# One standing PSUM tile for the products of the update stage

## The chip, the cores and the metric

The kernel runs on one core of one Trainium2 chip. The metric is device time in microseconds from the start to the end of one execution. Engines are named as in the profile: PE (TensorE, with PEld for its weight loads), DVE (VectorE), ACT (ScalarE), POOL (GpSimd) and SP (SyncE, which issues most transfers).

## What is computed

Two layers of a graph network over 6250 nodes with 160 features (64 scalars and 32 vectors of three components) and 100,000 edges sorted by their target node. In each layer every edge makes a message from its source node's features, and the messages are summed per target node. The first layer ends with an update of each node by a full tensor product of its own features with the summed messages, and the change lies in that update:

```python
def _tp(x0, x1, y0, y1, w000, w011, w101, w110):
    out0 = (jnp.einsum('eu,ev,uvw->ew', x0, y0, w000)
            + INV_SQRT3 * jnp.einsum('euk,evk,uvw->ew', x1, y1, w110)) / np.sqrt(fan0)
    out1 = (jnp.einsum('eu,evk,uvw->ewk', x0, y1, w011)
            + jnp.einsum('euk,ev,uvw->ewk', x1, y0, w101)) / np.sqrt(fan1)
...
agg = jax.ops.segment_sum(msgs, row, num_segments=N)
a0, a1 = _split(agg)
x0, x1 = _split(node_features)
u0, u1 = _tp(x0, x1, a0, a1, wu000, wu011, wu101, wu110)
ud0, ud1 = _lin(x0, x1, lu0, lu1)
return node_features + _merge(u0 + ud0, u1 + ud1)
```

## The kernel before

The program has three stages, one after the other. scatter() makes the first layer's messages and writes them to DRAM in the order of their source bins. update() sums them per node, computes the tensor product above and prepares the tables of the second layer. windows() does the second layer. A fourth part, general(), is for inputs that don't fit the layout; it isn't executed here.

update() takes the nodes in 13 groups, twelve of 500 and one of 250, with the nodes of a group along the free axis. Its order on PE, DVE, ACT and POOL is the order in which the code issues the instructions (manual_schedule, line 952); each engine works its own list in order, and engines wait for each other through semaphores only. The framework derives those waits itself: from a tile pool, whose slot is given to a new tile when all users of the old one are done, and from the overlap of what instructions read and write in one tile.

For each group there are 32 **rounds**, listed in plan (lines 784 to 787): 8 of kind y, 16 of kind x and 8 of kind v. Sorted by their times they come as y, x, v, x, and so on. A round is Group.first (lines 828 to 863):

- It takes a PSUM tile y of 128 partitions and two banks (line 832), from the pool py, which has two such slots (line 636). So rounds alternate between two slots, four banks in all.
- PE makes two products, one into each bank. In a y round they are two fp32 matmuls on half the rows each (line 835), in an x or v round two bf16 matmuls with a one-hot matrix that repeats rows of x (line 854).
- DVE multiplies them by the summed messages a. In a y round there are two instructions (line 839): the first reads bank 0 three times over, the second bank 1. In an x or v round one instruction reads both banks (line 857). The results go to SBUF (pr, pr2).
- POOL adds what belongs together (lines 842 and 862); line 824 makes a part of the v rounds' sums ahead of time.

The result of a round is multiplied by the weights and summed on PE in out0 and out1 some rounds later (Group.second, line 870; an x round's 2 rounds later, a y round's 4, a v round's 8). Between the rounds, the loop at lines 972 to 1000 puts in pieces of two other jobs: the segment sums of the next group (sums, lines 696 to 759, with PE at lines 735 and 751) and the end of the group before (back, lines 877 to 949, with PE at lines 896, 897, 932, 942 and 943, and DVE at lines 900 to 914). A group's first two sums are opened by begin (lines 806 and 807).

PSUM has eight banks, and update() uses all: four for y, two for out0 and out1 (pool pu), two for the other jobs (pool pt).

Of the kernel before, what the change touches and what calls it, by code (L numbers as in the profile page):

```python
# [13 lines left out]
F32 = mybir.dt.float32  # L14
# [6 lines left out]
PSUM = bass.MemoryType.PSUM  # L21
DRAM = bass.MemoryType.DRAM

P = 128
# [32 lines left out]
def gnn_kernel(ctx: ExitStack, tc: tile.TileContext, a: dict, out: bass.AP):  # L57
# [565 lines left out]
    def update():  # L623
# [3 lines left out]
        with ExitStack() as s:  # L627
# [5 lines left out]
            prod = s.enter_context(tc.tile_pool(name="prod", bufs=4))  # L633
            pair = s.enter_context(tc.tile_pool(name="pair", bufs=5))
            pprod = s.enter_context(tc.tile_pool(name="pprod", bufs=2))
            py = s.enter_context(tc.tile_pool(name="py", bufs=2, space=PSUM))
            pu = s.enter_context(tc.tile_pool(name="pu", bufs=1, space=PSUM))
            pt = s.enter_context(tc.tile_pool(name="pt", bufs=2, space=PSUM))
            f0, f1 = 1.0 / math.sqrt(5120.0), 1.0 / 64.0
# [137 lines left out]
                return x0, x1, x1k, x3, v3  # L777

            halves = (slice(0, M0), slice(M0, P))

# [7 lines left out]
            class Group:  # L790
# [37 lines left out]
                def first(self, kind, c):  # L828

                    n, a = self.n, self.a  # L830
                    x0, x1, x1k, x3, v3 = self.side
                    y = py.tile([P, 2, 4 * P], F32, name="y")
                    if kind == "y":
                        for i, (half, rhs) in enumerate(zip(halves, (x0[:, :n], a[halves[1], 0, :n]))):
                            nc.tensor.matmul(y[:, i, :n], w1[half, c], rhs, start=True, stop=True)  # L835
                        prs = []
                        for i, other in enumerate((a[:, 1:, :n], x1k[:, :, :n])):
                            pr = prod.tile([P, 3, 4 * P], F32, name="pr")
                            nc.vector.tensor_tensor(pr[:, :, :n], y[:, i, None, :n].to_broadcast([P, 3, n]), other,  # L839
                                                    op=OP.mult)  # L840
                            prs.append(pr[:, :, :n])
                        nc.gpsimd.tensor_tensor(prs[0], prs[0], prs[1], op=OP.add)  # L842
                        return [(prs[0], 1, [(slice(M1 * k, M1 * k + M1), s1[:, 28 - 4 * c:][:, :M1])
                                             for k in range(3)])]
                    if kind == "v":
                        k, c = c
                    for i in range(2):
                        if kind == "x":
                            u = 2 * (c + i)
                            w, rhs = pick[:, u % M1:u % M1 + 2], x3[:, u // M1, :n]  # L850
                        else:
                            u = 4 * (c + i)
                            w, rhs = pickv[:, u:u + 4], v3[:, k, :n]
                        nc.tensor.matmul(y[:, i, :n], w.rearrange("p i v -> p (i v)"), rhs, start=True, stop=True)  # L854
                    pr = pair.tile([P, 2, 4 * P], F32, name="pr2")
                    j = 0 if kind == "x" else 1 + k
                    nc.vector.tensor_tensor(pr[:, :, :n], y[:, :, :n], a[:, j, None, :n].to_broadcast([P, 2, n]),  # L857
                                            op=OP.mult)
                    if kind == "x":
                        return [(pr, 0, list(zip(halves, (w000[:, c], w000[:, c + 1]))))]  # L860
                    pp = self.early[c]
                    nc.gpsimd.tensor_tensor(pp[:, :, :n], pp[:, :, :n], pr[:, :, :n], op=OP.add)  # L862
                    return [(self.early.pop(c), 0, list(zip(halves, (w110[:, c], w110[:, c + 1]))))] if k else []
# [819 lines left out]
    with tc.tile_pool(name="early", bufs=1) as pool:  # L1683
        e = early(pool)
        update()
        windows(e)
# [93 lines left out]
```

## Time and profile before

| | |
|---|---|
| median of 17 runs | 3767.79 us (3754.69 to 3779.67) |
| the profiled execution | 3761.49 us, span 3759.6 us |
| first and last instruction on tile y | 1406.2 and 2325.4 us |
| busy between 1405 and 2327 us | PE 829.4, DVE 704.3, POOL 680.7, ACT 371.3 us |
| granted clock of PE, in that stretch and in all | 0.97 and 0.744 |
| L854 matmuls (x and v rounds), median | 374 ns, 624 of them |
| L835 matmuls (y rounds), median | 579 ns, 416 of them |
| L839 readings (y rounds), median | 1721 and 1710 ns, 104 each |
| L857 readings (x and v rounds), median | 1192 ns, 312 |

Times are counted from the start of the span. A reading here is an instruction of DVE that reads y. An fp32 matmul appears as two entries in the trace, so the 208 matmuls of the y rounds are 416. The last group's instructions are half as wide and shorter than these medians. The clock is given as the share of full speed that PE was granted.

### The profile page before, as it was taken

What the parts mean: (1) busy time and instruction counts of PE and PEld (TensorE: products, weight loads), DVE (VectorE), ACT (ScalarE), POOL (GpSimd) and SP (SyncE); (2) the same over time, 40 slices, a digit from 0 to 9 for tenths busy, and PEclk for the clock granted to TensorE, in tenths of its full rate; (3) what the DMA queues carried; (4) which work ended last, traced back from release to release, by engine and by line L of the source; (5) the groups of instructions that cost most, each with busy time, mean ns of one, the idle gap of its engine ahead of it and who ended that gap; (6) DMA issues with size and microseconds to landing.
All of it is one profiled execution on the core that took longest, in us unless ns stands there. A gap on an engine that the chain in (4) does not pass through costs nothing.

```text
span 3759.6 us, 47528 instructions
## 1 busy us (share of the span) xinstructions
PE 2384.6 (63%) x11860; PEld 1250.4 (33%) x11860; DVE 2219.7 (59%) x4577; ACT 1525.1 (41%) x5063; POOL 2221.2 (59%) x1864
## 2 busy tenths in 40 slices
PE   5655565565544437989898998455555555655555
PEld 3433343343333322333333333132323223332323
DVE  6665555555444437867777785455555556555554
ACT  3554544454444423443443441333433333333333
POOL 3655556555666636767777776655555555555552
PEclk7777777676666658999999998566656676566656
DMA  5655555465444456666566642445444454445442
GB/s 163 180 167 163 154 161 174 148 170 152 136 131 129 136 180 179 185 191 177 172 197 192 171 136 73 131 130 147 131 136 135 131 146 134 132 134 147 133 134 74
DMA packets 352776, 563.34 MB, mean 150 GB/s; under 512 B 66034, under 2 KB 251824, under 8 KB 346603
## 3 DMA queue, kind: packets, MB, share of 16 engines
q1 hardware_dynamic: 235496, 296.85, 28.6%
q0 software_dynamic: 87584, 218.31, 19.7%
q10 hardware_dynamic: 29411, 45.06, 3.7%
q8 instruction: 96, 1.57, 0.2%
q14 instruction: 189, 1.55, 0.1%
HBM read 418.16 MB, written 133.04 MB: 147 GB/s over the span
## 4 chain that ended last, share of the span: by engine, by line
PE 23%; another core or an unknown queue 21%; ACT 15%; DVE 14%; issue 12%; DMA 7%; SPq 5%; POOL 2%; ACTq 1%; DVEq 0%; POOLq 0%
ACT wm L1093 4%; ACT junk L556 4%; PE pmsg L545 3%; PE out L870 3%; DVE pr L839 2%; PE wbank L1150 2%; PE wbank L1218 2%; PE rank L544 2%; DVE wtb L1107 2%; PE rank L543 2%; ACT uhot L719 2%; PE wgate L1081 2%; PE y L835 1%; DVE wm L1117 1%
## 5 line engine op out<-in xcount | busy, mean ns | idle before, releaser
L563 POOL DMA_INDIRECT msgs<-rec,pos_i x782 | 782.8, 1001 | 568.4 <-issue 220.3
L1062 POOL DMA_INDIRECT wgot<-T,src_i x782 | 741.5, 948 | 636.4 <-issue 425.7
L543 PE MATMUL rank<-seen,every 128*128 128x256 f16 x782 | 265.0, 339 | 459.5 <-ACT junk L556 367.6
L556 ACT ACTIVATE junk<-rank,off 128x256 bf16<-128x256 f32 x782 | 373.6, 478 | 387.7 <-remote 289.5
L545 PE MATMUL pmsg<-tw,d 120*128 120x160 f32 x1564 | 470.8, 392 | 68.7 <-issue 54.9
L1081 PE MATMUL wgate<-wrad,wblk 97*128 97x480 f32 x522 | 367.6, 836 | 173.4 <-issue 140.8
L842 POOL TENSOR_TENSOR pr<-pr 128x1500 f32<-128x1500 f32 (+1 forms) x104 | 338.0, 3250 | 155.0 <-DVE pr L839 155.0
L857 DVE TENSOR_TENSOR pr<-y,a 128x1000 f32<-128x1000 f32 (+1 forms) x312 | 352.3, 1154 | 101.4 <-PE y L854 100.9
L1099 DVE TENSOR_TENSOR whot<-lane,wbank 128x192 f32<-128x192 f32 x131 | 45.9, 350 | 619.7 <-ACT wbank L1207 552.2
L1218 PE MATMUL wbank<-wms,whot 128*32 128x160 f32 x1564 | 250.1, 404 | 208.6 <-ACT wo L1222 105.3
L545 PEld LDWEIGHTS pmsg<-tw,d 120*128 120x128 f32 x1564 | 322.6, 256 | 137.2 <-issue 79.5
L1093 ACT ACTIVATE wm<-wgot,wattr 128x160 f32<-128x160 f32 x782 | 311.6, 398 | 34.7 <-DMA wgot<-T,src_i 10.8
L560 DVE CAST pos_i<-pos 128x4 int32<-128x4 f32 x196 | 42.9, 219 | 401.9 <-ACT junk L556 376.9
L1096 ACT ACTIVATE wsg<-wgate 128x480 f32<-128x480 f32 x259 | 137.4, 567 | 350.0 <-remote 189.5
L544 PEld LDWEIGHTS <-upto 128*128 128x128 bf16 x782 | 93.0, 119 | 552.6 <-issue 508.4
L1218 PEld LDWEIGHTS wbank<-wms,whot 128*32 128x32 f32 x1564 | 144.5, 142 | 395.4 <-ACT wo L1222 136.4
L862 POOL TENSOR_TENSOR ppr<-ppr,pr 128x1000 f32<-128x1000 f32 (+1 forms) x104 | 232.3, 2234 | 70.3 <-DVE pr L857 70.2
L531 DVE TENSOR_TENSOR seen<-seen,hot 128x256 f16<-128x256 f16 x782 | 230.5, 295 | 63.2 <-DVE hot L528 18.6
L544 PE MATMUL rank<-hot,upto 128*128 128x256 bf16 x782 | 266.4, 341 | 1.1 <-DVE hot L528 1.1
L528 DVE TENSOR_SCALAR hot<-binb,qb 128x256 bf16<-128x256 bf16 x782 | 243.7, 312 | 0.0
L839 DVE TENSOR_TENSOR pr<-y,a 128x1500 f32<-128x1500 f32 (+1 forms) x104 | 172.5, 1659 | 98.4 <-PE y L835 69.6
L1081 PEld LDWEIGHTS wgate<-wrad,wblk 97*128 97x128 f32 x522 | 128.1, 278 | 307.5 <-issue 242.6
(214 smaller groups left out, 4430.4 us busy)
## 6 DMA issues: line engine op xcount, KB each, us to landing
urec<-msgs SPq DMA_DIRECT2D x250, 322.0 KB
attb<-in_attr SPq DMA_DIRECT2D x48, 960.0 KB
tw<-T0s SPq DMA_DIRECT2D x391, 75.0 KB
xb<-hT SPq DMA_DIRECT2D x192, 125.0 KB
dstb<-in_dstrow SPq DMA_DIRECT2D x48, 480.0 KB
T0s<-tt ACTq DMA_DIRECT2D x11, 1200.0 KB
msgs<-rec,pos_i POOLq DMA_INDIRECT x782
wgot<-T,src_i POOLq DMA_INDIRECT x782
```

Of the source, the lines that this page charges most:

```text
L543: nc.tensor.matmul(rank[:, j % 2], every, before, start=True, stop=False)
L544: nc.tensor.matmul(rank[:, j % 2], upto, hot, start=False, stop=True)
L545: nc.tensor.matmul(prs[-1][:, j % 2, :F], ds[j // WP][:, j % WP], tws[j // WP], start=True, stop=True)
L556: nc.scalar.activation(junk, rank, AF.Relu, bias=off, accum_out=pos[:, j:j + 1])
L563: nc.gpsimd.indirect_dma_start(out=views[(t0 + j) % NV][:, :], out_offset=bass.IndirectOffsetOnAxis(ap=pos_i[:, j:j + 1], axis=0), in_=rec ...
L839: nc.vector.tensor_tensor(pr[:, :, :n], y[:, i, None, :n].to_broadcast([P, 3, n]), other, op=OP.mult)
L842: nc.gpsimd.tensor_tensor(prs[0], prs[0], prs[1], op=OP.add)
L857: nc.vector.tensor_tensor(pr[:, :, :n], y[:, :, :n], a[:, j, None, :n].to_broadcast([P, 2, n]), op=OP.mult)
L1062: nc.gpsimd.indirect_dma_start(out=got[u][:, i], out_offset=None, in_=T1[:, :], in_offset=bass.IndirectOffsetOnAxis(ap=src_i[:, t0 + i:t0 ...
L1081: nc.tensor.matmul(p[:, :n], blocks[u // CH][:, u % CH], rad[:, lo * F:lo * F + n], start=True, stop=True)
L1093: nc.scalar.activation(m[:, b, j:j + F], g[:, i, oS1:oS1 + F], AF.Copy, scale=attr(u)[:, i, 0:1])
L1218: nc.tensor.matmul(state["acc"][j:j + WN], hot[:, i], ms[:, i], start=t0 + i == w * WT, stop=t0 + i == end, tile_position=(0, j))
```

## The change

The pool py gets one slot in place of two, and one tile of four banks is taken from it before the rounds begin. A round takes the first or the second two banks of that tile in turn, where before it took a new tile from the pool. Matmuls, readings and their order are the same, and so is the number of banks.

```diff
-            py = s.enter_context(tc.tile_pool(name="py", bufs=2, space=PSUM))
+            py = s.enter_context(tc.tile_pool(name="py", bufs=1, space=PSUM))
...
             halves = (slice(0, M0), slice(M0, P))
+            ys, turn = py.tile([P, 2, 2, 4 * P], F32, name="y"), [0]
...
                     x0, x1, x1k, x3, v3 = self.side
-                    y = py.tile([P, 2, 4 * P], F32, name="y")
+
+                    y = ys[:, turn[0] % 2]
+                    turn[0] += 1
                     if kind == "y":
```

## The prediction

> **What bounds the kernel now.** I read the page first: the engines' shares, then the slices, then the stretch in which the changed tile lives.
>
> ```profile
> PE 2384.6 (63%) x11860; PEld 1250.4 (33%) x11860; DVE 2219.7 (59%) x4577; ACT 1525.1 (41%) x5063; POOL 2221.2 (59%) x1864
> ...
> PE   5655565565544437989898998455555555655555
> ...
> DVE  6665555555444437867777785455555556555554
> ...
> PEclk7777777676666658999999998566656676566656
> ```
>
> No engine is full over the span, but slices 16 to 24 stand out: PE at nine tenths, DVE at seven to eight, the clock at 0.9. That is the update stage. The instructions on tile y run from 1406.2 us to the last reading at 2325.4 (0.65 long): 919.8 us. Nothing of the next stage's compute runs beside it, so a microsecond more in it is a microsecond more in the span.
>
> Then the waits in that stretch (engine, line, what it waited for: us, times, longest):
>
> ```profile
> DVE pr L857 <- PE y L854: 100.9, 94, 4.2
> DVE pr L839 <- PE y L835: 69.6, 71, 3.1
> ...
> PE y L854 <- DVE pr L839: 32.6, 40, 10.2
> PE y L835 <- DVE pr L857: 12.8, 21, 0.8
> ```
>
> PE and DVE hold each other up: DVE waits 170.5 us for products, PE waits for DVE to empty a buffer. The stage is a loop of the two, and what it costs depends on how far PE may run ahead. The timeline shows that (start, duration, engine, line):
>
> ```profile
> 1860.40 0.58 PE L854 MATMUL y<-x,pick 96*128 96x500 bf16 x2
> ...
> 1861.03 1.20 DVE L857 TENSOR_TENSOR pr<-y,a 128x1000 f32<-128x1000 f32 x1 [0.89 <-PE y L854]
> ...
> 1861.91 0.68 PE L835 MATMUL y<-x,w_f 64*128 64x500 f32 x1
> ...
> 1862.95 1.04 PE L870 MATMUL out<-pr,s 128*32 128x500 f32 x6
> ...
> 1863.13 1.72 DVE L839 TENSOR_TENSOR pr<-y,a 128x1500 f32<-128x1500 f32 x1 [0.91 <-PE y L835]
> ...
> 1863.92 0.59 PE L854 MATMUL y<-x,pick 96*128 96x500 bf16 x2
> 1864.44 1.06 PE L870 MATMUL out<-pr,w_f 128*64 128x500 f32 x4
> ...
> 1864.77 1.71 DVE L839 TENSOR_TENSOR pr<-y,x1k 128x1500 f32<-128x1500 f32 x1
> ...
> 1866.40 1.19 DVE L857 TENSOR_TENSOR pr<-y,a 128x1000 f32<-128x1000 f32 x1
> ...
> 1866.54 0.59 PE L854 MATMUL y<-v,pickv 96*128 96x500 bf16 x2 [0.29 <-DVE pr L839]
> ```
>
> At 1863.92 PE makes the next round's products while DVE reads the y round's (1863.13 to 1866.48); so DVE goes on at 1866.40 without a gap. Two rounds on, the v round's matmuls (1866.54) wait for both readings.
>
> **The change, step by step.** It adds no computing instruction and removes none. The same four banks are used; what changes is who waits for whom.
>
> *1. What the bookkeeping sees.* Before, each round's y is a tile of its own from a pool of two. After, all 416 rounds use one tile, and the order is kept by the overlap of accesses inside it. So the question is whether two accesses to different banks of one PSUM tile count as overlapping. Three facts of the program before say yes. In a y round the first L839 reads bank 0 alone, yet it waits for the count raised by the second matmul, which writes bank 1 (in 80 of 104 rounds the first matmul raises no count at all). The second L839, which alone needs bank 1, has no wait on PE. And in wm, the other two-bank tile, each L1093 into the second bank is ordered behind those into the first. Both are two-bank tiles; none of four exists before. I take it that a PSUM tile is ordered as a whole.
>
> *2. The wait that follows.* Then the two halves of the standing tile are no double buffer. The first matmul of a round waits for the last reading of the round just before, not of the one two rounds back. Behind it on PE's queue stand all L870 sums, the segment sums (L735, L751) and the transposes; DVE waits for the products. Products and readings strictly alternate. From the timeline: a y round is 1.22 us from first matmul to first reading (1861.91 to 1863.13), 3.35 of readings (to 1866.48), 0.06 until PE starts again: 4.63. An x or v round is 0.63 (1860.40 to 1861.03), 1.20 and 0.06: 1.89. Four rounds y, x, v, x: 4.63 + 3 x 1.89 = 10.30. There are 104 such fours; in the last group eight have 250 columns, and from their shortest rows (readings 0.94, 0.93 and 0.65) I estimate 6.0. Sum 96 x 10.30 + 8 x 6.0 = 1036.8, which is **117 us** over the 919.8.
>
> *3. Waits the alternation doesn't hold.* DVE also waited for transfers: 17.9 us for a at the start, 21.6 for uxo, 9.2 for x1k. The first stays, the others shrink as rounds get longer and the DMA does not: between 18 and 49, I take **30**.
>
> *4. PE late.* In an x round PE is done with the products 0.52 us after their start (1863.92 to 1864.44) and needs 0.99 for its L870 pair (to 1865.43); 0.38 of the 1.89 is left. Segment sums come as sets of 1.23 us, 58 of them, two fifths in the first x round: 23 x 0.85 = 20. The group's opening matmuls (L806, L807: 1.9 us) come in a v round, 13 x 1.0 = 13; a few of L942 and L943 besides. I take **40**. The ends: 0, and 120, if three fifths of those lines' 265 us came late but for the 0.38s. POOL is no limit: 3.25 + 2.23 + half of 2.24 is 6.6 per four rounds.
>
> *5. PE's clock.* While DVE reads a y round, PE has its own L870 sums (to 1863.99) and then nothing of the rounds until 1866.48: a hole of 2.49 us. What such a hole does can be read in the trace (stretch: PE busy, PEld, DVE, ACT, POOL, clock, DMA share, GB/s):
>
> ```profile
> 1616.70:1620.10 3.40, 1.24 (x10) 1.07 (x11) 2.45 (x2) 0.53 (x2) 2.29 (x2) 1.00 0.55 198
> 1620.10:1623.60 3.50, 3.50 (x14) 1.92 (x16) 0.59 (x1) 2.12 (x4) 2.47 (x1) 0.51 0.46 117
> ...
> 2087.80:2091.20 3.40, 1.25 (x7) 0.66 (x7) 2.21 (x3) 0.00 (x0) 0.63 (x1) 1.00 0.67 122
> 2091.20:2094.60 3.40, 3.40 (x30) 1.33 (x32) 3.26 (x4) 0.00 (x0) 3.40 (x2) 0.50 0.02 5
> ```
>
> The clock changes on a grid of 3.4 us; where PE was busy for 1.25 of a cell, the next ran at half. The hole behind the second was 2.50 us (L896 waiting for L900). The stage has eight such drops, after cells with 0.9 to 2.1 of 3.4 busy, while cells with 1.96 and 1.91 (from 1838.6 and 2057.0) kept the clock. So a cell with over 1.5 us of hole drops. A hole of 2.49 thrown on the grid puts that much into one cell in (0.92 + 1.98) / 3.41 = 85% of the cases. Some 60 of the 104 y rounds have no segment sums or transposes to fill the hole; with some of the filled ones I take 65 drops. In a half-speed cell an x round needs 1.04 + 2.0 = 3.0 us of PE instead of 1.89, so 3.41 us do 1.1 rounds and not 1.8: 1.3 us lost; as the clock came back only after a cell that was busy throughout, 1.7 cells each, 2.2 us. 65 x 2.2 = **143**. The ends: 0 (the eight drops of now), and 104 x 2.5 = 260.
>
> The Trainium skill (TensorE: Matmul & The Clock Gate, "Why this matters for your kernels") warns only of PE-idle gaps above about 3 us. By that rule a hole of 2.49 would cost nothing and the sum would end near 3955; the 2.50 us hole above speaks against it, and the row decides.
>
> *6. What is saved.* Even with the whole tile ordered, nothing: no wait of before becomes shorter, since the round just before always ends later than the one two back.
>
> **Sum.** 117 + 30 + 40 + 143 = 330. The profiled execution took 3761.5 us for a span of 3759.6: 3761.5 + 330 = 4091.5. The median of the runs, 3767.8, is 6 above it: **4098**, and I write 4100.
>
> **Rivals.**
>
> *A. The banks are freed one by one (faster).* The price is in the v rounds only: x and v rounds read both banks with one instruction, a y round with two. The v round's first matmul could start 1.65 us earlier (1864.77 instead of 1866.48), the second not. So PE saves at most one matmul's spacing, 0.22 to 0.30, in the rounds in which it waited: 94 by PE's and PEld's counts (40 and 54), 21 to 28 us; half of it, where the next x round waits for its own buffer anyway (0.51 at 1867.64), 12. Time 3768 - 20 = 3748. It decides as soon as accesses to different banks of a tile are kept apart. For it: at 1863.92 a matmul and a reading run side by side in different banks, so the chip allows it. Against: step 1. Chance 0.04.
>
> The Trainium skill (PSUM — Partial Sum Buffer, "Summary: rules for kernel authors") says to read PSUM beside a matmul from a different bank and to guard it by bank. By that the sum would be this rival's 3748; the waits in this program are coarser than the rule.
>
> *B. The slots stay apart, the banks in one do not.* Then every wait is as before: 3768. No tile of four banks exists before, so I can't exclude it. Chance 0.05.
>
> *C. Whole tile, but the clock holds*, because sums and transposes fill the holes or the grid treats them kindly: steps 2 to 4 alone, 117 + 30 + 40 = 187, with up to 60 of step 5: 3955 to 4015. Chance 0.28.
>
> *Forecast*, whole tile with the clock falling often: 0.63.
>
> **How the numbers follow.** Low end: steps 2 and 3 with their least, 117 + 18, and a little of step 4: 3768 + 155, 3920. High end: 117 + 49 + 80 + 225, 4240. Forecast and C lie mostly within, A and B (0.09) outside, and perhaps a tenth of the rest. A measurement of this kernel can tell about 0.2%, 7.5 us, from no change. Faster: A, 0.04. Same: B, 0.05. Slower: 0.91.
>
> **What would show it.** Right: in the stage no L854 or L835 starts before the last reading of the round before has ended; DVE's wait for y grows from 170 to 300 us or more; four rounds take 10.3 us or more where none is filled; the clock of the stage falls from 0.97 to 0.75 or 0.85; the stages before and after stay as long. Wrong: matmuls still run under L839 (A or B); a v round's first matmul starts between the two readings (A); the clock stays above 0.95 (C). If the stage grows by far more than 400 us, PE is late more often than in step 4.

## The result and the profile after

The changed kernel takes **4060.51 us** (median of 8 runs, 4041.92 to 4066.79) against 3764.52 for the kernel before on the same chips: a ratio of 1.0782, 95% interval [1.0766, 1.0798]. The prediction was 4100, range 3920 to 4240. The profiled execution has a span of 4053.4 us, 293.8 more than before. The tile y is in use from 1413.3 to 2621.6 us, 1208.3 us in place of 919.8, so 288 us of the difference lie in the update stage; the stretch ahead of it is 7.1 us longer than before and the one behind it 1.8 shorter.

The lines of its page that answer to those of before; three lines of code were added, so lines from 833 on have numbers higher by 3, those from 780 to 831 by 1:

```profile
PE 2486.1 (61%) x11860; PEld 1278.8 (32%) x11860; DVE 2237.0 (55%) x4577; ACT 1521.5 (38%) x5063; POOL 2218.4 (55%) x1864
...
PE   5555555654444367777777777735566555655556
...
DVE  6655554554444355655666656535555555555554
...
PEclk7766777666666688888889988856666666666666
```

The counts of instructions are the same. The stage now fills slices 14 to 25, and in it all three rows are lower than before: PE at seven tenths and not nine, DVE at five to six, the clock at 0.8 to 0.9. Nothing got more work; the engines wait more. (PE's total rises by 101 us with the same matmuls, since those at half clock last longer: four of L873 took 1.93 us at 1900.15, in a stretch at half clock, and 1.06 at 1906.78.)

The waits in the stage (engine, line, what it waited for: us, times, longest):

```profile
DVE pr L860 <- PE y L857: 300.5, 300, 4.2
DVE pr L842 <- PE y L838: 149.2, 94, 3.1
...
PE y L857 <- DVE pr L842: 141.4, 94, 11.9
PE y L857 <- DVE pr L860: 93.7, 130, 1.7
```

Before, the last of these was:

```profile
PE y L854 <- DVE pr L857: 8.3, 18, 0.5
```

DVE waited for x and v products 94 times before; now it does in 300 of 312 rounds, three times as long. PE's matmuls wait for the readings of an x or v round 130 times, where it was 18 times. The timeline shows the new order:

```profile
1906.27 0.58 PE L857 MATMUL y<-x,pick 96*128 96x500 bf16 x2
...
1906.96 1.20 DVE L860 TENSOR_TENSOR pr<-y,a 128x1000 f32<-128x1000 f32 x1 [1.50 <-PE y L857]
...
1908.21 0.68 PE L838 MATMUL y<-x,w_f 64*128 64x500 f32 x1 [0.37 <-DVE pr L860]
...
1909.37 1.72 DVE L842 TENSOR_TENSOR pr<-y,a 128x1500 f32<-128x1500 f32 x1 [1.21 <-PE y L838]
...
1911.01 1.71 DVE L842 TENSOR_TENSOR pr<-y,x1k 128x1500 f32<-128x1500 f32 x1
...
1912.77 0.58 PE L857 MATMUL y<-x,pick 96*128 96x500 bf16 x2 [2.48 <-DVE pr L842]
...
1913.39 1.20 DVE L860 TENSOR_TENSOR pr<-y,a 128x1000 f32<-128x1000 f32 x1 [0.67 <-PE y L857]
```

The x round's reading ends at 1908.16, the y round's matmuls start at 1908.21; the last y reading ends at 1912.72, the next x matmuls start at 1912.77. No matmul on y lies under a reading any more. The hole is there too: PE stood for 2.48 us before 1912.77 (2.49 in the prediction).

### The profile page after: what moved, and what is told of

The parts are those of the page before. It is cut to its first block, busy times and chain, and to the rows that moved or that the text cites. A ratio compares the mean times of both kernels' runs of the same rounds, so it can differ in the third digit from the quotient of the medians.

```text
span 4053.4 us, 47424 instructions
## 1 busy us (share of the span) xinstructions
PE 2486.1 (61%) x11860; PEld 1278.8 (32%) x11860; DVE 2237.0 (55%) x4577; ACT 1521.5 (38%) x5063; POOL 2218.4 (55%) x1864
## 4 chain that ended last, share of the span: by engine, by line
PE 30%; DVE 23%; another core or an unknown queue 19%; issue 11%; ACT 10%; DMA 3%; SPq 2%; POOL 1%; ACTq 1%; DVEq 0%; POOLq 0%
DVE pr L842 8%; DVE pr L860 6%; PE y L857 4%; PE out L873 4%; PE pmsg L545 4%; ACT wm L1096 3%; ACT junk L556 3%; PE y L838 3%; PE wbank L1221 2%; PE wbank L1153 2%; PE rank L544 2%; PE wgate L1084 2%; PE rank L543 2%; DVE wtb L1110 2%
## 5 line engine op out<-in xcount | busy, mean ns | idle before, releaser
L860 DVE TENSOR_TENSOR pr<-y,a 128x1000 f32<-128x1000 f32 (+1 forms) x312 | 361.7, 1159 | 300.5 <-PE y L857 300.5
L857 PE MATMUL y<-x,pick 96*128 96x500 bf16 (+1 forms) x416 | 128.4, 392 | 221.1 <-DVE pr L842 141.4
L873 PE MATMUL out<-pr,w_f 128*64 128x500 f32 (+1 forms) x832 | 243.3, 667 | 0.0
```

The costliest lines, as they stand in the source:

```text
L873: nc.tensor.matmul(out[part, :self.n], w, pr[:, i, :self.n], start=k in self.fresh, stop=self.left[k] == 0)
```

## The experiments

The theory: accesses are ordered by the whole PSUM tile, so one standing tile of four banks is a single buffer, and the loss is the alternation of products and readings, PE coming late in short rounds, and PE's clock. Rivals: that a standing tile as such costs time; that banks do overlap and something else is slow; that the clock costs nothing. A drop below is a stretch in which PE was granted half of its clock, and half-speed time is the sum of these stretches in the stage. The views have the line numbers of each run's own kernel; the text uses those of the kernel before, where it doesn't say otherwise.

### Two standing tiles

```diff
-            ys, turn = py.tile([P, 2, 2, 4 * P], F32, name="y"), [0]
+            ys, turn = [py.tile([P, 2, 4 * P], F32, name=f"y{i}") for i in range(2)], [0]
...
-                    y = ys[:, turn[0] % 2]
+                    y = ys[turn[0] % 2]
```

> The four banks stand as two tiles of two banks each, taken once and used in turn; no slot is ever given back, as in the change. Theory (accesses are ordered by the whole PSUM tile, so what hurts is that both halves are one tile): the waits are those of before, the y stage is 920 us and the time 3765 us, within 0.3%. Rival (standing tiles as such cost time, whatever their number, because no slot is released): 4060 us as with the change. Third possibility: something between, if standing tiles and the joint order both count.

Measured: 3766.27 us, ratio to before 0.9998 [0.9977, 1.0020]. The waits in its stage:

```profile
DVE pr L860 <- PE y L857: 99.7, 92, 4.3
DVE pr L842 <- PE y L838: 71.0, 71, 2.7
...
PE y L857 <- DVE pr L842: 34.6, 40, 11.9
```

They are those of before, to a microsecond or two. The banks, the order of instructions and the standing are as in the change; only the border between two tiles is new, and with it the whole loss is gone. The first rival falls.

### One slot

```diff
-            py = s.enter_context(tc.tile_pool(name="py", bufs=2, space=PSUM))
+            py = s.enter_context(tc.tile_pool(name="py", bufs=1, space=PSUM))
```

This is the kernel before with half the PSUM for y and no other edit.

> The kernel before with one slot in the pool py in place of two, so a plain single buffer of two banks. Theory (the change amounts to a single buffer): the same time as the change, 4060 us within 0.5%, stage 1208 us with about 40 clock drops. Rival (the change still overlaps some bank with some reading): the single buffer is slower than the change by 20 us or more, some 0.2 us in each of 104 y rounds.

Measured: 4049.01 us, ratio 1.0759 [1.0716, 1.0802], which holds the change's 1.0782. Its stage is 1197.5 us with 40 clock drops (the change: 1208.3 and 41).

```profile
DVE pr L857 <- PE y L854: 296.2, 300, 4.2
DVE pr L839 <- PE y L835: 138.4, 92, 3.2
```

A plain single buffer of two banks waits as the change does with four. So the other two banks buy nothing, and no bank of the standing tile is freed ahead of another to any use.

### Filling PE's hole with narrow matmuls, six and three

```diff
+                        for _ in range(6):
+                            nc.tensor.matmul(side1[0][V:, :n], pick[:, 0, :M1], x3[:, 0, :n], start=True, stop=True,
+                                             tile_position=(0, V))
                         prs = []
```

side1[0] is the group's out1, made 128 partitions high; the matmuls are added work into its unused quarter.

> The change, with six matmuls more in each y round, into a quarter of the out1 bank that nothing reads, issued just behind the y round's two products: some 1.3 us of PE work in the 2.49 us hole that PE has while DVE reads. Theory (part of the loss is PE's clock, lost in those holes): half-speed time in the stage falls from 271 us to under 80 us, and the time by 70 to 140 us, to 3920 to 3990 us, although PE does more. Rival (the clock drops fall into time in which PE waits anyway and cost nothing; all of the loss is the alternation): 4060 us or a little more.

> As with six, but three more matmuls, some 0.65 us: the hole shrinks to about 1.85 us. Theory (a 3.4 us cell of the clock's grid with over 1.5 us of hole drops): between the change and the run with six, half-speed time 130 to 230 us, time 4000 to 4050 us. Rival (only holes near 2.5 us and longer drop the clock): three do as much as six. Rival without a clock term: 4060 us.

Measured: 4044.56 us, ratio 1.0759 [1.0708, 1.0809], with six, and 4054.92, 1.0788 [1.0743, 1.0833], with three; half-speed time 259 and 317 us. Both are like the change, and neither theory is tested: the narrow matmuls ran beside the L870 sums and filled almost nothing. In the run with six, the y round of this stretch still left PE 2.04 us idle where it was 2.48.

### Filling it with full-width matmuls, six and nine

```diff
             halves = (slice(0, M0), slice(M0, P))
+            spare = pf.tile([P, 4 * P], F32, name="spare")
...
+                        for _ in range(6):
+                            nc.tensor.matmul(spare[:, :n], pick[:, 0:2].rearrange("p i v -> p (i v)"), x3[:, 0, :n],
+                                             start=True, stop=True)
                         prs = []
```

These stand on the one-slot kernel, which leaves two PSUM banks free; the tile spare is one of them and nothing reads it.

> The kernel with one slot (4049 us, half-speed time 242 us, 40 drops) plus six matmuls of full width in each y round, into one of the two PSUM banks that it leaves free and that nothing reads. The earlier fillers were a quarter wide and ran beside L870, so the hole stayed at 2.0 us; these can't, and cut it from 2.49 to some 1.1 us. Theory (lost clock is part of the loss): half-speed time under 100 us and 50 to 110 us less time, 3940 to 4000 us, with more work done. Rival (the drops cost nothing, or the added matmuls cost as much as the clock gives): 4049 us or more.

> The same with nine matmuls, 2.0 us, which fill the hole nearly whole. Theory: the clock holds (half-speed time under 60 us), but in the y rounds with segment sums or transposes PE now comes late by up to 1 us: 3950 to 4030 us, no better than with six. Rival (no clock term): slower than one slot alone by 10 to 60 us.

Measured: 4041.14 us, ratio 1.0740 [1.0722, 1.0758], with six; 4059.33, 1.0772 [1.0749, 1.0795], with nine. Half-speed time fell from 242 to 140 and 91 us, less far than expected (under 100 and under 60), and the time hardly moved. By itself that would speak for the rival. But the rounds of the trace show a second effect: in the first x rounds at full clock PE came 0.06 us after the last reading with one slot, 0.43 with six and 0.78 with nine, because in y rounds that hold segment sums there was no hole left. 90 rounds by 0.37 is 33 us. Gain and loss are mixed; the pair alone is inconclusive.

### Filling only the empty holes

The same matmuls, seven of them, at the end of a y round, and only where the loop put no segment sums or transposes in. The count at building time was 41 of 104 rounds.

```diff
+                    if kind == "y" and not busy[0]:
+                        for _ in range(7):
+                            nc.tensor.matmul(spare[:, :gs[g].n], pick[:, 0:2].rearrange("p i v -> p (i v)"),
+                                             gs[g].side[3][:, 0, :gs[g].n], start=True, stop=True)
+                    busy[0] = 0
```

> One slot, with seven matmuls of full width only at the end of those y rounds into which the loop puts no segment sums or transposes: 41 of 104. So they lie in a hole of 2.49 us and delay nothing, which those of the runs with six and nine did not (x rounds came 0.4 to 0.7 us late there). Theory (the clock costs what the half-speed rounds are longer than the others, 53 us in the profile of one slot): half-speed time from 242 us to 80 to 140, time 25 to 50 us under one slot's 4049, 4000 to 4025 us. Rival (the drops cost nothing): 4049 us. Second rival (they cost the 2.2 us each of the prediction): below 3990 us.

Measured: **3983.11 us**, ratio 1.0584 [1.0558, 1.0610], against 1.0759 for one slot: more work on PE and 66 us less time. Between the two profiled executions it is 63.2 us, of which 51.6 lie in the stage; the rest lies in the stretches around it, where the kernels don't differ. The stage by stretches (length, busy PE, PEld, DVE, ACT, POOL, clock, DMA share, GB/s), first one slot, then with the empty holes filled:

```profile
1411.00:2610.00 1199.00, 923.01 (x5258) 311.29 (x5256) 723.70 (x676) 370.45 (x1361) 682.49 (x260) 0.90 0.45 129
```

```profile
1408.00:2555.00 1147.00, 923.12 (x5550) 321.79 (x5550) 723.66 (x676) 370.95 (x1364) 682.74 (x260) 0.96 0.46 135
```

PE has some 290 matmuls more and is busy just as long, since they run at a higher clock (0.96, not 0.90). Drops fell from 40 to 17, half-speed time from 242 to 92 us, the stage from 1197.5 to 1145.9: 51.6 us for 23 drops, **2.2 us a drop**. That is more than the theory's 25 to 50 us, which came from comparing half-speed rounds with others (perhaps a slow round also delays the round behind it; this isn't shown). The second rival held: 2.2 us a drop, and a time below its 3990. The clock costs time; the first rival falls. The price comes from one pair of profiled executions, but it also fits the runs with six and nine. Six: 12 drops fewer are 27 us less, the 90 late rounds 33 more, so the stage should be 6 us longer than with one slot, and it is 4 (1201.6). Nine: 22 drops fewer are 49 less, 95 late rounds by 0.73 are 69 more, so 20 longer, and it is 19 (1216.5).

### Single banks that really come free one by one

```diff
-            py = s.enter_context(tc.tile_pool(name="py", bufs=2, space=PSUM))
+            py = s.enter_context(tc.tile_pool(name="py", bufs=4, space=PSUM))
...
-                    y = py.tile([P, 2, 4 * P], F32, name="y")
+                    y = [py.tile([P, 4 * P], F32, name="y") for _ in range(2)]
...
-                    nc.vector.tensor_tensor(pr[:, :, :n], y[:, :, :n], a[:, j, None, :n].to_broadcast([P, 2, n]),
-                                            op=OP.mult)
+                    for i in range(2):
+                        nc.vector.tensor_tensor(pr[:, i, :n], y[i][:, :n], a[:, j, :n], op=OP.mult)
```

The control has the split readings (the last lines) on the two-bank tiles of before.

> Four PSUM tiles of one bank each, two per round, and the one reading of an x or v round split into one per bank, so that the banks really come free one by one. Theory (the joint order of the tile is all that stood in the way; the first rival of the prediction named 12 to 28 us for it): faster than the kernel with two-bank tiles and split readings by 20 to 60 us, as each matmul waits for the reading of its own bank alone; against the kernel before, whose readings are not split, 3720 to 3775 us. Rival (PE and DVE are so coupled that the earlier bank gains nothing): the same as the control within 0.3%.

> The control: the kernel before with its two-bank tiles in two slots, only the one reading of each x and v round (1.19 us) split into one per bank (0.65 us each by the half-width rows, so 0.1 us more per round, 31 us in 312 rounds). Theory: DVE, which waits for PE 170 us in the stage, hides part of it: 3765 to 3800 us. Rival (the split costs in full and the second reading also delays the slot's release): 3800 us or more.

Measured: single banks 3772.92 us, ratio 1.0028 [1.0016, 1.0040]; control 3769.05, 1.0017 [1.0000, 1.0034]. The theory's 20 to 60 us are not there, and the rival holds: the earlier bank gains nothing. PE's waits, first with single banks, then in the control:

```profile
PE ptr L896 <- DVE uxo L900: 29.5, 17, 5.1
PE y L854 <- DVE pr L839: 20.1, 17, 9.9
```

```profile
PE y L854 <- DVE pr L839: 33.1, 37, 11.7
...
PE ptr L896 <- DVE uxo L900: 12.9, 10, 4.5
```

The wait for the y readings does shrink, from 37 times to 17, but behind L900, which waits for the transfer of uxo, PE now stands 16.6 us longer. That suggests the gain was given back there, which the next pair was to test.

### Loading the nodes' rows earlier

```diff
+                    if r == 24:
+                        gs[g].rows()
...
-                    xo = pool.tile([P, 4, F], F32, name="uxo")
-                    transfer(nc.sync, xs, xo, r0, n)
-                    yield
+                    xo = self.xo
+                    yield
```

rows() takes the tile uxo and loads it. The first run is the kernel before with this edit, the second has the single banks too.

> The kernel before, only the load of the nodes' rows (uxo) issued in round 24 of its own group and not when the group's end begins. Control for the next run. DVE waited 21.6 us for that transfer, PE 10.1 behind it. Theory (that wait is on the loop of PE and DVE): 3735 to 3755 us. Rival (PE or DVE waits somewhere else instead): 3765 us within 0.2%.

> Four one-bank tiles with split readings, and the early load of the rows. With four tiles alone PE's wait for the y readings fell from 33.1 to 20.1 us against the control, but the wait for uxo rose from 25.4 to 36.9 us on DVE and from 12.9 to 29.5 on PE. Theory (what the banks give is given back at that transfer): with the load early it shows, 15 to 40 us less than the early load alone, 3705 to 3735 us, faster than both kernels. Rival (the loop gains nothing from single banks, and pays for the split): the same as the early load alone, or up to 15 us more.

Measured: 3782.97 us, ratio 1.0051 [1.0034, 1.0069], with the early load alone, and 3774.24, 1.0036 [1.0019, 1.0053], with single banks too. Both expectations of a gain were wrong, and the early load alone is even slower than its rival said (within 0.2%). PE's waits with the early load alone:

```profile
PE ptr L945 <- ACT utt L950: 38.4, 10, 4.1
PE y L858 <- DVE pr L843: 32.3, 38, 10.3
```

The wait for uxo is gone from the list, but PE now waits 38.4 us for ACT's copies of utt, which take the last results of the group's end out of PSUM (6.1 before), and DVE's wait for products rises from 170 to 212 us. Whether the banks' gain went to the uxo wait therefore stays open: taking that wait away made another. Single banks were worth nothing without the early load; with it they are 9 us below, but the two intervals overlap, and the 15 to 40 us of the theory are not there.

### Moving PE's other work into the y rounds

```diff
-                    for _ in range((2, 2, 0, 1)[r % 4] if r >= 3 and g + 1 < len(groups) else 0):
+                    for _ in range((4, 0, 0, 1)[r % 4] if r >= 3 and g + 1 < len(groups) else 0):
...
-                    for _ in range((1, 2, 0, 1)[r % 4]):
+                    for _ in range((3, 0, 0, 1)[r % 4]):
```

> The change, with the two pieces of segment sums and the two of the group's end that the loop issues in each first x round moved to the y round before it; nothing else. So PE has them in the hole of 2.49 us and not in the 0.4 us that an x round leaves. Theory (PE late is a term of its own, some 44 us in the v rounds that follow those x rounds, and the clock drops come of empty y rounds): the time before the matmuls of those v rounds falls from 0.68 us to near 0.1, fewer y rounds are empty, drops fall from 41 to under 25: 40 to 90 us less than the change, 3970 to 4020 us. Rival (the moved pieces wait for each other, for ACT's copies of ptr, and PE stands in order behind them): no gain, 4050 us or more.

Measured: 4190.03 us, ratio 1.1130 [1.1108, 1.1152], so 130 us slower than the change. The moved effect is as expected where it was aimed: at full clock the v rounds' matmuls now come 0.14 us after the last reading, not 0.68. But the rival is right about the whole:

```profile
PE ptr L945 <- ACT utt L950: 90.0, 20, 9.0
```

```profile
1906.47 8.53 SPq L693 DMA_DIRECT2D urec<-msgs  x8
...
1915.11 7.40 SPq L951 DMA_DIRECT2D T<-utt  x4
1919.16 0.48 ACT L950 COPY utt<-ptr 128x384 f32<-128x384 f32 x1 [9.45 <-DMA T<-utt]
...
1919.69 0.70 PE L945 MATMUL ptr<-w_fn,uT 64*116 64x96 f32 x2 [8.79 <-ACT utt L950]
```

Issued one behind the other, the end pieces wait for ACT's copy, the copy for the transfer of an earlier piece, and all that stands behind on PE waits too. The rival didn't name one link: that transfer began to be issued only at 1915.11, since from 1906.47 to 1915.00 SyncE issued the eight loads of urec that the moved segment sums ask for. Drops rose to 63.

## Why the prediction was right

**The bookkeeping (step 1)** was right, and on it all else hung: two tiles give 0.9998, one slot gives the change's time. The chance of 0.91 for slower rested on a reading of two-bank tiles only; for four banks the same holds.

**The terms of the sum** against what the trace and the runs give:

| | predicted, us | measured, us |
|---|---|---|
| alternation (step 2) | 117 | 107 |
| waits for transfers (step 3) | 30 | 11 |
| PE late (step 4) | 40 | 65 |
| PE's clock (step 5) | 143 | 92 |
| sum | 330 | 275 |
| the stage's growth | | 288 |

- *Alternation.* At full clock a y round is 1.18 + 3.35 + 0.05 = 4.58 us and an x round 0.62 + 1.20 + 0.05 = 1.87, so a four 10.19; a half-size four is 6.03. 96 and 8 of them make 1026.5, 107 over 919.8.
- *Transfers.* DVE waits 17.8 us for a, once. The stage's first matmul starts at 1413.3 and its reading at 1425.7, 12.4 us for the usual 1.2, so 11 us of it are added to the alternation. The nine waits for x<-hX (11.6 us, 1.29 each) add next to nothing: 1.21 us is what DVE waits in a y round anyway. Those for x1k and uxo are gone.
- *PE late.* In the rounds at full clock, the time from the last reading to the first matmul is 80.6 us in sum over 315 rounds, 65 beyond the usual 0.05 each. 44 of it is in the full-size v rounds behind the first x rounds, where step 4 had put only the segment sums (20 us).
- *Clock.* **This was the mis-sized term.** The price of a drop was right (2.2 us predicted and measured). The number was not: 41 drops for the 65 predicted. Two parts of that count failed. "Some 60 of the 104 y rounds have no segment sums or transposes": it is 41. And a hole of 2.49 us was to cost a drop in 85% of the cases: filling those 41 holes took away 23 of 40 drops, 56%. As the 1026.5 us hold no drop, all 41 count, and 41 by 2.24 us are 92. The price was measured on the one-slot kernel and is carried over.

Of the 13 us that are left of the stage's growth, about 10 are in the v and second x rounds: their time from matmul to reading is 0.06 to 0.08 us longer than in the first x rounds. The 92 can be held against the change's own trace: the 101 rounds that half speed touches between the reading before and their own are 96 us longer in sum than the alternation gives (the wait for a apart), of which some is PE late.

**Too much on the clock, the transfers and the alternation and too little on PE late** cancelled in part, so the forecast lay only 40 us high; that is luck. Of the signs named, DVE's wait for y came (449.7 us in sum), and two missed by little: an unfilled four takes 10.19 us, not 10.3 or more, and the stage's clock is above the forecast's.

**Nothing saved (step 6)** fits: no term of the growth is negative. **Rival A** was wrong not only in its condition but in its price: with banks apart, 12 to 28 us were named, and none appeared. **Rival B** is ruled out by the result, since two banks apart from the other two would have left 3768. **Rival C** was nearer than its chance of 0.28 says: the stage's clock is 0.89, between its 0.95 and the forecast's 0.75 to 0.85, and 4060 lies between its 4015 and the forecast.

**The rule that step 5 names from the Trainium skill** (TensorE: Matmul & The Clock Gate, "Why this matters for your kernels": no PE-idle gap above about 3 us) would have given 3955. Holes of 2.5 us did drop the clock here, and the stage was 51.6 us shorter when the empty ones were filled, so the row of the trace was the better guide.

## What to carry to other kernels

Before merging buffers into one standing PSUM tile, look at what the program orders by: if a reader of one bank waits for the writer of another bank of its tile, the tile is the unit, and two tiles of the same banks keep the overlap that one tile loses. When two engines come to alternate, count not only the gap between them but also what the idle engine's other work does, late in short rounds and missing in long ones, and whether the holes cost it its clock. A wait that is taken away in a loop of several engines may come back somewhere else, so its length is no forecast of the gain.

## What the runs showed of the hardware

- In the prediction's rows PE's clock fell to half after a 3.4 us cell with a hole of 2.50 us, and each drop cost 2.2 us of time in the one-slot stage. Not every such hole did it: filling 41 of them took 23 drops away. And half-speed time is not all lost time: 150 us less of it (242 to 92) made the stage 51.6 us shorter.
- A matmul of 32 columns into one quarter of the partitions runs beside matmuls into the others: six of them left 2.04 us of a hole of 2.48.
- Splitting a reading of 128x1000 into two of 128x500 cost DVE little: two took 1.26 us together at 1909.39 with single banks, one whole one 1.19.
